# Softmax sums and the RMS factor carried to the free axis through one compact tile of bf16 parts

## The chip, the cores and the metric

The kernel runs on one core of a Trainium2 chip. The metric is the time of one execution on the device in microseconds, the median of several executions. TensorE (PE) multiplies matrices, VectorE (DVE), ScalarE (ACT) and GpSimd (POOL) do elementwise work, and SyncE (SP) issues all DMA transfers from one queue. "PEld" in the profile is TensorE's loading of weights.

## The reference

Four graph layers run over 32 independent graphs (batches) of 512 nodes with 256 features. Each layer is followed by a residual sum and a layer norm.

```python
# layer 0: attention with 8 heads of 32, masked by the adjacency
scores = where(adj > 0, q @ k.T / sqrt(32), NEG)
x = ln(x + (softmax(scores) @ v) @ Wo + bo)
# layer 1
h = (1 + eps1) * x + adj @ x
x = ln(x + relu(h @ W11 + b11) @ W12 + b12)
# layer 2
h = (eps2 * x + adj @ x) @ W21 + b21              # 1024 wide
h = h * rsqrt(mean(h ** 2, -1) + 1e-6) * rms_w
x = ln(x + silu(h) @ W22 + b22)
# layer 3
xn = layernorm(x) * gamma + beta
L  = I - s_out[:, None] * adj * s_in[None, :]      # s: 1 / sqrt(degree)
x  = ln(x + softplus(xn @ W_self + L @ xn @ W_neigh))
```

All data is fp32. The two places of this change are the division by the softmax sums (one sum for each node and head) and the multiplication by the RMS factor (one for each node).

## The kernel before, in words

One graph's 512 nodes are four tiles of 128 rows (NT = 4), its 256 features two tiles of 128 (DC = 2), and four heads share a tile of 128 features (HPG = 4). For each graph the function `graph` records its operations, stage by stage: the transposed loads of adjacency and x (`adjT`, `xT`), `qk`, `v`, the attention of four heads at a time (`attend(0)`, `attend(1)`), `wo` and the layer norm, then the first layer's `agg1`, `w11`, `w12`, the second's `agg2`, `w21`, `rms`, `silu`, `w22`, and the last layer's `x3T`, `pz`, `lap` and `softplus`.

The names that the steps below use:

- `sc` (L766): scores of four heads for 128 nodes, four matmuls of 32 rows each, in the form 32*128. L790 (DVE) masks them and finds the row minima, L804 (ACT) takes the exponential and writes its row sums to `rs`. L840 (DVE) transposes blocks in place, and L852/L864 (SP) move the tile `pq` out to DRAM (`via`) and back as `pT`.
- `po_att` (L883): probabilities times v for a pair of node tiles, 128*32 form. It holds the unnormalised result with features on partitions and nodes on the free axis.
- stage `rinv` (L903 to L957): the sums lie with nodes on partitions, and are needed along the free axis. The reciprocal `rv` (L903) is split into three bf16 parts (L912, L919), set into a zeroed 128-column tile `parts` for each node tile, transposed by four TensorE transposes (`pm_t`, L930), copied to SBUF (`mT`, L937/L938), and spread over each head's 32 partitions by one bf16 matmul of 512 columns with a selector (`pr_r`, L943). The result is copied to `oT` (L532/L533) and multiplied with `po_att` (L955). This runs once for each of the two groups of heads.
- `wo`: the matmuls `po<-wo,oT` (L970). Of two matmuls for a node tile, the second reads the second group's `oT`.
- `adjT` in graphs after the first: four loads (L580), two block transposes on VectorE (L614), a pass for the degrees on ScalarE (L624). Two buffers of adjT alternate, so a graph's loads wait for `lap` (`pa_l`, L1411) of the graph two before.
- `pg` (L1165) is the 1024-wide product of layer 2, copied by VectorE (L1220) or ScalarE (L1226); ScalarE squares it (L1241) and GpSimd adds the squares up (`ssq`, L540).
- stage `rms`: `pm` (L1251) sums the squares over partitions with nodes on the output's partitions, L1263 makes the mean, GpSimd the power -1/2 (`rr`, L558). Four VectorE products of the identity with `rr` make diagonal tiles `diag` (L1275), and one fp32 matmul of 512 columns with a matrix of ones spreads them (`pb`, L1281). Eight VectorE operations multiply by it (L1289).

The order of the work is not the order of recording. The class `Order` is a planner: each recorded operation carries a cost and, sometimes, two ways (VectorE or ScalarE). `Order.run` places operations greedily, engine by engine. An operation's rank is its due time:

```python
keys[o.n] = b * period + d - (self.HASTE if b == max(by_b) else 0)
```

Here `d` mixes the earliest and latest start within one graph (weight `LATE`) and adds `LEAD[stage]`, a number for each stage. The planner knows the buffers of each pool (four PSUM banks of tag "m"), the cost `TURN` of a change of array form on TensorE, and that VectorE operations marked `port` and GpSimd's long operations exclude each other. What it returns is emitted in that order, so several graphs are interleaved on each engine, and each engine then runs its own queue in order.

Of the kernel before, what the change touches and what calls it, by code (L numbers as in the profile page):

```python
# [9 lines left out]
F32 = mybir.dt.float32  # L10
BF16 = mybir.dt.bfloat16
AF = mybir.ActivationFunctionType
ALU = mybir.AluOpType
# [3 lines left out]
P = 128  # L17
# [2 lines left out]
RMS_EPS = 1e-6  # L20
HEADS = 8

PERIOD = 55957
LEAD = {
    "adjT": 178900, "agg1": 2600, "agg2": -164100, "degree": 73600, "diag": -115600,
# [4 lines left out]
}  # L30


# [27 lines left out]
class Order:  # L60
# [8 lines left out]
    WAIT = 70  # L69
    TABLE, TABLE_DUE = 1300, 9000  # L70

    TURN = {"whole": 93, "row": 200, "col": 93}
    TURN_DUE = 6000
    LATE = 0.85
    HASTE = 12445

    def __init__(self):
        self.ops = []
# [204 lines left out]
def kernel(  # L283
# [53 lines left out]

    ident_b = const.tile([P, P], BF16, name="ident_b")  # L340
    nc.vector.tensor_copy(ident_b, ident)
    parts = []
    for i in range(2):
        t = const.tile([P, NT, P], BF16, name=f"parts{i}")
        nc.gpsimd.memset(t, 0.0)
        parts.append(t)
    id_js = ident.rearrange("p (j s) -> p j s", s=HD)
    block = const.tile([P, HPG], F32, name="block")
    nc.vector.tensor_reduce(block, id_js, axis=AX.X, op=ALU.add)
    rows_js = const.tile([P, HPG], F32, name="rows_js")  # L350
    nc.vector.tensor_reduce(rows_js, id_js[:, :, 0:3], axis=AX.X, op=ALU.add)
    rows_of = const.tile([P, 1], F32, name="rows_of")
    nc.vector.tensor_reduce(rows_of, rows_js, axis=AX.X, op=ALU.add)
    sel_r = const.tile([P, HPG, HD], BF16, name="sel_r")
    nc.vector.tensor_scalar_mul(
        sel_r, block.unsqueeze(2).to_broadcast([P, HPG, HD]), rows_of[:, 0:1]
    )

    order = Order()

# [138 lines left out]
    def graph(b):  # L499
# [26 lines left out]
        def either(r, w, dve_way, act_way, port=False):  # L526
            op([("DVE", dve_way[0], dve_way[1], {"port": 1} if port else {}), ("ACT", act_way[0], act_way[1], {})], r, w)
# [32 lines left out]
        def small(name, bufs=2, shape=None):  # L560
            return Buf(sb, shape or [P, NT], F32, "s_" + name, f"{name}_{b}", bufs)
# [186 lines left out]

        oT = tmp([P, DC, N], "oT", 1)

        def attend(g):


            mx = small("mx", 2, [P, NT, HPG])
            rs = small("rsum", 2, [P, NT, HPG])
            po = bank("po_att")
            pTs = []
            for t in range(NT):
# [21 lines left out]
                for j in range(HPG):  # L780

                    if early:
                        row = lambda pq=pq, j=j: pq().rearrange(
                            "p a j c s -> p (a j c s)"
                        )[:, j * N : (j + 1) * N].rearrange("p (a n) -> p a n", a=4)
                    else:
                        row = lambda pq=pq, j=j: pq[:, :, j].rearrange("p a c s -> p a (c s)")
                    dve(
                        780,
                        lambda t=t, j=j, sc=sc, row=row: nc.vector.tensor_tensor_reduce(  # L790
                            out=row(),
                            in0=sc[:, j, :].rearrange("p (a n) -> p a n", a=4),
                            in1=bias[:, t, :].rearrange("p (a n) -> p a n", a=4),
                            scale=-1.0,
                            scalar=3.0e38,
                            op0=ALU.add,
                            op1=ALU.min,
                            accum_out=mx[:, t, j : j + 1],
                        ),
                        [(sc, j), (bias, t)], [(pq, j), (mx, t, j)],  # L800
                    )
                    act(
                        800,
                        lambda t=t, j=j, row=row: nc.scalar.activation(  # L804
                            row(), row(), AF.Exp,
                            bias=mx[:, t, j : j + 1],
                            scale=-1.0,
                            accum_out=rs[:, t, j : j + 1],
                        ),
                        [(mx, t, j)], [(pq, j), (rs, t, j)],  # L810
                        table="exp",
                    )
                stage[0] = "move"
# [81 lines left out]
                )  # L895

            stage[0] = "rinv"

            tj = [(t, j) for t in range(NT) for j in range(HPG)]
            rv = small("rv", 2, [P, NT, HPG])  # L900
            dve(
                240,
                lambda: nc.vector.reciprocal(rv(), rs()),  # L903
                [(rs, t, j) for t, j in tj], [(rv,)],
            )
            part = parts[g].rearrange("p t (j s) -> p t j s", s=HD)
            left = rv
            for r in range(3):
                dst = part[:, :, :, r]
                dve(  # L910
                    190,
                    lambda dst=dst, left=left: nc.vector.tensor_copy(dst, left()),  # L912
                    [(left,)], [("parts", g), ("parts", g, r)], port=True,
                )
                if r < 2:
                    rest = small("rest", 2, [P, NT, HPG])
                    dve(
                        180,
                        lambda dst=dst, left=left, rest=rest: nc.vector.tensor_tensor(  # L919
                            rest(), left(), dst, ALU.subtract  # L920
                        ),
                        [(left,), ("parts", g, r)], [(rest,)], port=True,
                    )
                    left = rest
            pm_t = Buf(ps, [P, N], BF16, "m", f"pm_t_{b}", 4)
            mT = tmp([P, N], "mT", 2, dtype=BF16)

            def tr():
                for t in range(NT):
                    nc.tensor.transpose(  # L930
                        pm_t[:, t * P : (t + 1) * P], parts[g][:, t, :], ident_b
                    )

            pe(240, tr, [("parts", g)] + [("parts", g, r) for r in range(3)], [(pm_t,)], mT)
            either(
                [(pm_t,)], [(mT,)],
                (420, lambda: nc.vector.tensor_copy(mT(), pm_t())),  # L937
                (590, lambda: nc.scalar.copy(mT(), pm_t())),  # L938
            )
            pr_r = bank("pr_r")  # L940
            pe(
                130,
                lambda: nc.tensor.matmul(  # L943
                    pr_r(),
                    lhsT=sel_r.rearrange("p j e -> p (j e)"),
                    rhs=mT(),
                    start=True,
                    stop=True,
                ),
                [(mT,)], [(pr_r,)], oT,  # L950
            )
            evacuate(lambda: oT[:, g, :], pr_r, [(pr_r,)], [(oT, g)])
            dve(
                700,
                lambda: nc.vector.tensor_tensor(oT[:, g, :], po(), oT[:, g, :], ALU.mult),  # L955
                [(po,)], [(oT, g)],
            )  # L957

        def pair_sum(lhs, lhs_k, w, w_k, nk, y, step):

# [101 lines left out]
        values()  # L1062
        attend(0)
        attend(1)
        stage[0] = "wo"
        pair_sum(oT, lambda k: (oT, k), wo, "wo", DC, y, DC)

# [211 lines left out]
        pe(  # L1279
            870,  # L1280
            lambda: nc.tensor.matmul(  # L1281
                pb(), lhsT=ones, rhs=diag().rearrange("p t q -> p (t q)"), start=True, stop=True
            ),
            [(diag,)], [(pb,)],
        )
        for m in range(C2):
            dve(
                750,
# [235 lines left out]
```

## Time and profile before

| | us |
|---|---|
| median of three runs | 3435.14 (3434.87 to 3435.78) |
| the profiled execution | 3424.53 |
| its span, first to last instruction | 3422.5 |
| VectorE busy in the span | 2664.6 |
| ScalarE busy | 2033.0 |
| GpSimd busy | 857.9 |
| TensorE granted clock | 0.998 |

Instructions of the two steps in the profiled execution (mean length of a record; records of consecutive matmuls overlap):

| line, engine | what | count | mean ns |
|---|---|---|---|
| L930 PE | pm_t, 128x128 bf16 | 256 | 219 |
| L943 PE | pr_r, 128x512 bf16 | 64 | 379 |
| L1281 PE | pb, 128x512 fp32, two passes | 64 | 639 |
| L903 DVE | reciprocal | 64 | 214 |
| L912 DVE | parts, of rv and of the rest | 64 and 128 | 637 and 185 |
| L919 DVE | rest | 128 | 175 |
| L938 ACT | mT from pm_t | 59 | 585 |
| L533 ACT | oT from pr_r | 61 | 586 |
| L955 DVE | oT times po_att | 64 | 688 |
| L1275 DVE | diag | 128 | 299 |

How to read the profile's lines: the groups give line, engine, operation, out<-in by the program's names, count, then busy time, mean length and idle time before. In the timeline the first two numbers are start and length in us, "x20" is a merged run of twenty, and brackets give the idle time before and what ended it. In the waits the numbers are total us, times and longest. An fp32 matmul of the program stands as two records (two passes). "32*128" is the form of the array, rows by columns.

### The profile page before, as it was taken

Reading aid. Unit: us, or ns where it says so; the run is one execution under the profiler, and the core shown is the slowest. Engines: PE = TensorE matmul, PEld = TensorE weight load, DVE = VectorE, ACT = ScalarE, POOL = GpSimd, SP = SyncE. Lnnn points to the kernel's source line nnn. Section 1 sums busy time; section 2 is a strip of 40 time slices with the busy share of each in tenths; the row PEclk is TensorE's granted clock in tenths of the full one; section 3 lists DMA queues with packets and bytes.
Section 4 is the critical chain, followed back from the end, with each engine's and each line's share of the span. In section 5 each row is a group of like instructions: output and inputs, shape, how many; then the busy total and the mean of one; then the engine's idle time right before and its main releaser. Section 6 shows DMA issues by size and latency. Waiting matters only on the chain.

```text
span 3422.5 us, 55733 instructions
## 1 busy us (share of the span) xinstructions
PE 3368.0 (98%) x20000; PEld 2030.2 (59%) x20000; DVE 2664.6 (78%) x6241; ACT 2033.0 (59%) x4124; POOL 857.9 (25%) x615
## 2 busy tenths in 40 slices
PE   8999999999999999999999999999999999999997
PEld 5556655665655666556655655565566655565565
DVE  7788878778777788777787777887877877778755
ACT  6555666556666556666566655666565666556633
POOL 1222222222232222222132321222222223212231
PEclk9999999999999999999999999999999999999999
DMA  5777766667767667666677666676766767766710
GB/s 152 231 220 215 207 195 191 197 186 213 198 186 199 194 197 202 195 189 197 187 212 198 186 191 200 194 204 190 197 191 191 215 191 196 192 196 180 207 40 13
DMA packets 622868, 644.74 MB, mean 188 GB/s; under 512 B 410752, under 2 KB 446976, under 8 KB 590848
## 3 DMA queue, kind: packets, MB, share of 16 engines
q1 hardware_dynamic: 622592, 641.19, 66.9%
q8 instruction: 157, 2.57, 0.3%
q14 instruction: 119, 0.97, 0.1%
HBM read 364.27 MB, written 276.82 MB: 187 GB/s over the span
## 4 chain that ended last, share of the span: by engine, by line
PE 89%; DMA 5%; DVE 3%; issue 1%; SPq 1%; ACT 1%; POOL 0%; DVEq 0%; POOLq 0%
PE po L970 22%; PE ph L1148 13%; PE pg L1165 7%; PE sc L766 7%; PE pq L694 7%; PE pa L1165 7%; PE pz L1369 7%; PE pa_l L1411 6%; PE po_att L883 6%; DMA adjT<-in_adj_dram 4%; PE pv L735 3%; PE pb L1281 1%; PE pt L1341 1%; DVE pq L790 1%; PE pm L1251 1%
## 5 line engine op out<-in xcount | busy, mean ns | idle before, releaser
L804 ACT ACTIVATE pq<-pq,mx 128x512 f32<-128x512 f32 x1024 | 728.1, 712 | 255.9 <-DVE mx L790 161.0
L790 DVE CUSTOM_DVE_ANT_0 pq<-sc,bias 128x512 f32<-128x512 f32 x1024 | 664.0, 684 | 151.0 <-PE sc L766 95.3
L840 DVE STREAM_TRANSPOSE pq<-pq 128x2048 f32<-128x2048 f32 x248 | 572.2, 2307 | 82.7 <-ACT pq L804 82.5
L970 PE MATMUL po<-w,gT 128*128 128x256 f32 x2048 | 466.6, 381 | 0.5 <-ACT gT L1304 0.5
L1165 PE MATMUL pg<-hT,w 128*128 128x512 f32 x1024 | 465.9, 598 | 0.0
L970 PEld LDWEIGHTS po<-w,gT 128*128 128x128 f32 x2048 | 384.4, 190 | 88.8 <-issue 36.9
L540 POOL TENSOR_TENSOR ssq<-ssq,sq 128x512 f32<-128x512 f32 x220 | 281.1, 1278 | 292.1 <-ACT sq L1241 285.1
L1023 POOL TENSOR_TENSOR rstd<-ve,nhalf 128x4 f32<-128x4 f32 x132 | 143.7, 1089 | 767.9 <-DVE ve L1018 767.8
L1165 PEld LDWEIGHTS pg<-hT,w 128*128 128x128 f32 x1024 | 189.4, 190 | 218.6 <-issue 206.0
L766 PE MATMUL sc<-kT,qT 32*128 32x512 f32 x2048 | 292.1, 640 | 5.3 <-DVE nmr L1030 4.4
L883 PEld LDWEIGHTS po_att<-pT,v 128*32 128x32 f32 x8192 | 215.8, 110 | 94.9 <-issue 66.8
L883 PE MATMUL po_att<-pT,v 128*32 128x128 f32 x8192 | 250.2, 274 | 0.0
L1369 PE MATMUL pz<-wsn,xnT 128*128 128x512 f32 x512 | 236.7, 597 | 0.4 <-DVE xnT L1352 0.4
L540 POOL TENSOR_TENSOR sp<-sp,y 128x1024 f32<-128x1024 f32 x31 | 73.0, 2355 | 645.6 <-PE pg L1165 572.5
L1165 PE MATMUL pa<-hT,w 128*128 128x512 f32 x512 | 233.3, 599 | 0.3 <-DVE hT L532 0.3
L1148 PE MATMUL ph<-adjT,y_att 128*128 128x512 f32 x512 | 227.3, 596 | 1.4 <-DVE adjT L1130 1.4
L1148 PE MATMUL ph<-adjT,y 128*128 128x512 f32 x512 | 228.5, 598 | 0.0
L970 PE MATMUL po<-w,aT 128*128 128x256 f32 x1024 | 227.6, 379 | 0.0
L1411 PE MATMUL pa_l<-zy,adjT 128*128 128x256 f32 x1024 | 226.6, 379 | 0.0
L1411 PEld LDWEIGHTS pa_l<-zy,adjT 128*128 128x128 f32 x1024 | 194.5, 190 | 40.8 <-issue 15.5
L970 PEld LDWEIGHTS po<-w,aT 128*128 128x128 f32 x1024 | 192.0, 190 | 26.5 <-ACT pq L804 0.8
L804 ACT ACTIVATION_READ_ACCUMULATOR pq<-pq,mx 128x1 f32 x1024 | 191.9, 187 | 0.0
(150 smaller groups left out, 4991.6 us busy)
## 6 DMA issues: line engine op xcount, KB each, us to landing
via<-pq SPq DMA_DIRECT2D x992, 256.0 KB, 4.3
pT<-via SPq DMA_DIRECT2D x248, 1024.0 KB, 5.7
adj<-in_adj_dram SPq DMA_DIRECT2D x32, 1024.0 KB, 5.1
adjT<-in_adj_dram SPq DMA_DIRECT2D x124, 256.0 KB, 4.7
x<-in_x_dram SPq DMA_DIRECT2D x32, 512.0 KB, 3.9
xT<-in_x_dram SPq DMA_DIRECT2D x124, 128.0 KB, 4.1
out_dram<-sp SPq DMA_DIRECT2D x31, 512.0 KB, 5.2
w<-in_L_gnn_W_dram SPq DMA_DIRECT2D x2, 1024.0 KB, 6.5
```

What stands on the lines that cost most here:

```text
L540: lambda: nc.gpsimd.tensor_tensor(dst(), dst(), src(), ALU.add), {},
L694: nc.tensor.matmul(pq(), lhsT=w[:, c, m * P : (m + 1) * P], rhs=xT[:, c, :], start=(c == 0), stop=(c == DC - 1),)
L766: nc.tensor.matmul(sc[:, j, :], lhsT=qT[hp, g, t * P : (t + 1) * P], rhs=kT[hp, g, :], start=True, stop=True,)
L790: lambda t=t, j=j, sc=sc, row=row: nc.vector.tensor_tensor_reduce(out=row(), in0=sc[:, j, :].rearrange("p (a n) -> p a n", a=4), in1=bias[ ...
L804: lambda t=t, j=j, row=row: nc.scalar.activation(row(), row(), AF.Exp, bias=mx[:, t, j : j + 1], scale=-1.0, accum_out=rs[:, t, j : j + 1],),
L840: lambda pq=pq: nc.vector.transpose(pq().rearrange("p a j c s -> p (a j c s)"), pq().rearrange("p a j c s -> p (a j c s)"),),
L883: nc.tensor.matmul(po[j * HD : (j + 1) * HD, t * P : (t + 1) * P], lhsT=v[:, c, h * HD : (h + 1) * HD], rhs=pT[:, :, j, c, :], start=(c == 0),
L970: nc.tensor.matmul(po[:, i * D : (i + 1) * D], lhsT=lhs[:, k, t * P : (t + 1) * P], rhs=w[:, k, :], start=(i == 0 and k == 0), stop=(i == ...
L1148: nc.tensor.matmul(ph(), lhsT=xin[:, m, c * P : (c + 1) * P], rhs=adjT[:, m, :], start=(m == 0), stop=(m == NT - 1),)
L1165: nc.tensor.matmul(pa(), lhsT=w[:, c, m * P : (m + 1) * P], rhs=hT[:, c, :], start=(c == 0), stop=(c == DC - 1),)
L1369: nc.tensor.matmul(pz(), lhsT=xnT[:, c, t * P : (t + 1) * P], rhs=wsn[:, c, :], start=(c == 0), stop=(c == DC - 1),)
L1411: nc.tensor.matmul(pa[:, i * D : (i + 1) * D], lhsT=adjT[:, m, t * P : (t + 1) * P], rhs=zy[:, m, D : 2 * D], start=(m == 0), stop=(m == N ...
```

## The change

All sums of both head groups are kept in one tile `rs` [128, 2, 4, 4]. `po_att` is copied to `oT` as soon as it is done. After both groups, `normalise` takes one reciprocal of 32 columns, splits it into three bf16 parts side by side (96 columns), transposes them with one TensorE transpose, and spreads them by eight bf16 matmuls of 128 columns (four for each group), each with its own selector. The product then reads the spread sums from PSUM and `oT` from SBUF. For the RMS factor, `split` makes 12 columns of parts, one transpose gives 12 rows, and four bf16 matmuls of 128 columns over 12 rows take the place of `diag` and the fp32 matmul. The planner's parameters are others too, so all engines' orders are planned anew; among the results, the first load in the DMA queue is x, and the adjT loads and transposes stand elsewhere.

```diff
-PERIOD = 55957
+PERIOD = 71805
 LEAD = {
-    "adjT": 178900, "agg1": 2600, "agg2": -164100, "degree": 73600, "diag": -115600,
-    "lap": -139200, "ln0": -34000, "ln1": -303400, "ln2": 108900, "ln3": 310600, "load": 67000,
-    "move": -461200, "pv": -4100, "pz": -65900, "qk": 9400, "rinv": -98900, "rms": -72400,
-    "scores": -4600, "silu": 110900, "softplus": 52400, "v": 134300, "w11": 4200, "w12": -5600,
-    "w21": -3500, "w22": -9100, "wo": -16600, "x3T": -71100, "xT": -89500,
+    "adjT": 1500, "agg1": -8100, "agg2": -16500, "degree": 64500, "diag": 111900, "lap": -94700,
+    "ln0": 5100, "ln1": 18700, "ln2": 16800, "ln3": 26700, "load": 6200, "move": 1300,
+    "pv": 5300, "pz": 15400, "qk": 7900, "rinv": -300, "rms": 100, "scores": -700,
+    "silu": -28600, "softplus": 46100, "v": 28700, "w11": -34100, "w12": -56500, "w21": 5500,
+    "w22": -8500, "wo": -32400, "x3T": -25400, "xT": -36000,
 }
...
-    TURN = {"whole": 93, "row": 200, "col": 93}
-    TURN_DUE = 6000
-    LATE = 0.85
-    HASTE = 12445
+    TURN = {"whole": 93, "row": 290, "col": 150}
+    TURN_DUE = 7000
+    LATE = 1.06
+    HASTE = 24152
...
+            evacuate(lambda: oT[:, g, :], po, [(po,)], [(oT, g)])
+
+        def split(src, n, name):
+
+            parts = tmp([P, 3, n], "p_" + name, 2, name + "p", dtype=BF16)
+            left, left_k = src, []
+            for r in range(3):
+                dve(
+                    190,
+                    lambda r=r, left=left: nc.vector.tensor_copy(parts[:, r, :], left()),
+                    [(left,)], [(parts, r)], port=True,
+                )
+                if r < 2:
+                    rest = small(name + "rest", 2, [P, n])
+                    dve(
+                        180,
+                        lambda r=r, left=left, rest=rest: nc.vector.tensor_tensor(
+                            rest(), left(), parts[:, r, :], ALU.subtract
+                        ),
+                        [(left,), (parts, r)], [(rest,)], port=True,
+                    )
+                    left = rest
+            pm_t = Buf(ps, [P, P], BF16, "m", f"pm_t_{b}", 4)
+            mT = tmp([P, P], "mT_" + name, 1, dtype=BF16)
+            pe(
+                65,
+                lambda: nc.tensor.transpose(
+                    pm_t[0 : 3 * n, :], parts().rearrange("p r x -> p (r x)"), ident_b
+                ),
+                [(parts, r) for r in range(3)], [(pm_t,)], mT,
+            )
+            either(
+                [(pm_t,)], [(mT,)],
+                (220, lambda: nc.vector.tensor_copy(mT[0 : 3 * n], pm_t[0 : 3 * n, :])),
+                (330, lambda: nc.scalar.copy(mT[0 : 3 * n], pm_t[0 : 3 * n, :])),
+            )
+            return mT
+
+        def normalise():
...
+            mT = split(rv, NX, "sums")
+            for g in range(2):
+                pr_r = bank("pr_r")
+
+                def spread(g=g, pr_r=pr_r):
+                    for t in range(NT):
+                        x = (g * NT + t) * HPG
+                        nc.tensor.matmul(
+                            pr_r[:, t * P : (t + 1) * P],
+                            lhsT=sel_r[0 : 3 * NX, x : x + HPG].rearrange("p j e -> p (j e)"),
+                            rhs=mT[0 : 3 * NX],
+                            start=True,
+                            stop=True,
+                        )
+
+                pe(240, spread, [(mT,)], [(pr_r,)])
                 dve(
...
+                    700,
+                    lambda g=g, pr_r=pr_r: nc.vector.tensor_tensor(
+                        oT[:, g, :], pr_r(), oT[:, g, :], ALU.mult
+                    ),
+                    [(pr_r,)], [(oT, g)],
+                )
...
         attend(0)
         attend(1)
+        normalise()
...
-        diag = tmp([P, NT, P], "sq", 2, "diag")
-
-        def spread():
+        mT = split(rr, NT, "rms")
+        pb = bank("pb")
+
+        def spread_rms():
             for t in range(NT):
-                nc.vector.tensor_scalar_mul(diag[:, t, :], ident, rr[:, t : t + 1])
+                nc.tensor.matmul(
+                    pb[:, t * P : (t + 1) * P],
+                    lhsT=sel_t[0 : 3 * NT, t],
+                    rhs=mT[0 : 3 * NT],
+                    start=True,
+                    stop=True,
+                )
 
-        dve(880, spread, [(rr,)], [(diag,)])
-        pb = bank("pb")
-        pe(
-            870,
-            lambda: nc.tensor.matmul(
-                pb(), lhsT=ones, rhs=diag().rearrange("p t q -> p (t q)"), start=True, stop=True
-            ),
-            [(diag,)], [(pb,)],
-        )
+        pe(240, spread_rms, [(mT,)], [(pb,)])
```

The selectors `sel_r` and `sel_t` are made once, at the start, from the identity.

More of the change, by code (lines that the diff above doesn't have):

```diff
@@ L341, with selector @@
     nc.vector.tensor_copy(ident_b, ident)
[L342 to L356, printed above, removed]
-    )
+    def selector(n, wide, name):
+        of = const.tile([P, n], F32, name=f"{name}_of")
+        nc.vector.tensor_reduce(
+            of, ident[:, 0 : 3 * n].rearrange("p (r x) -> p x r", r=3), axis=AX.X, op=ALU.add
+        )
+        sel = const.tile([P, n, wide], BF16, name=name)
+        nc.vector.tensor_copy(sel, of.unsqueeze(2).to_broadcast([P, n, wide]))
+        return sel
+    NX = 2 * NT * HPG
+    sel_r = selector(NX, HD, "sel_r")
+    sel_t = selector(NT, P, "sel_t")
     order = Order()
@@ L749, in graph @@
         oT = tmp([P, DC, N], "oT", 1)
+        rs = small("rsum", 2, [P, 2, NT, HPG])
         def attend(g):
             mx = small("mx", 2, [P, NT, HPG])
-            rs = small("rsum", 2, [P, NT, HPG])
             po = bank("po_att")
@@ L807, in attend @@
                             scale=-1.0,
-                            accum_out=rs[:, t, j : j + 1],
+                            accum_out=rs[:, g, t, j : j + 1],
                         ),
-                        [(mx, t, j)], [(pq, j), (rs, t, j)],
+                        [(mx, t, j)], [(pq, j), (rs, g, t, j)],
                         table="exp",
@@ L897, in attend @@
             stage[0] = "rinv"
-            tj = [(t, j) for t in range(NT) for j in range(HPG)]
-            rv = small("rv", 2, [P, NT, HPG])
-            dve(
-                240,
-                lambda: nc.vector.reciprocal(rv(), rs()),
-                [(rs, t, j) for t, j in tj], [(rv,)],
-            )
[L906 to L909, printed above, removed]
-                dve(
-                    190,
-                    lambda dst=dst, left=left: nc.vector.tensor_copy(dst, left()),
-                    [(left,)], [("parts", g), ("parts", g, r)], port=True,
-                )
[L915 to L920, printed above, removed]
-                        ),
-                        [(left,), ("parts", g, r)], [(rest,)], port=True,
-                    )
-                    left = rest
@@ L925, in attend @@
[L925 to L939, printed above, removed]
@@ L940, in attend @@
-            pr_r = bank("pr_r")
-            pe(
[L942 to L957, printed above, removed]
+            evacuate(lambda: oT[:, g, :], po, [(po,)], [(oT, g)])
@@ new lines, in normalise @@
+        def normalise():
+            stage[0] = "rinv"
+            rv = small("rv", 2, [P, NX])
+            dve(
+                240,
+                lambda: nc.vector.reciprocal(rv(), rs().rearrange("p g t j -> p (g t j)")),
+                [(rs, g, t, j) for g in range(2) for t in range(NT) for j in range(HPG)],
+                [(rv,)],
+            )
+            mT = split(rv, NX, "sums")
[12 more added lines that the diff above has]
+                pe(240, spread, [(mT,)], [(pr_r,)])
+                dve(
+                    700,
[3 more added lines that the diff above has]
+                    [(pr_r,)], [(oT, g)],
+                )
@@ L1269, in graph @@
         rsqrt(rr, ms, [(ms,)], [(rr,)])
-        diag = tmp([P, NT, P], "sq", 2, "diag")
-        def spread():
+        mT = split(rr, NT, "rms")
+        pb = bank("pb")
+        def spread_rms():
             for t in range(NT):
-                nc.vector.tensor_scalar_mul(diag[:, t, :], ident, rr[:, t : t + 1])
-        dve(880, spread, [(rr,)], [(diag,)])
-        pb = bank("pb")
-        pe(
-            870,
-            lambda: nc.tensor.matmul(
-                pb(), lhsT=ones, rhs=diag().rearrange("p t q -> p (t q)"), start=True, stop=True
-            ),
-            [(diag,)], [(pb,)],
-        )
+                nc.tensor.matmul(
[6 more added lines that the diff above has]
+        pe(240, spread_rms, [(mT,)], [(pb,)])
         for m in range(C2):
```

## The prediction

> **What bounds the kernel now.** I read the page first: busy shares, the slices, the chain that ended last.
>
> ```profile
> PE 3368.0 (98%) x20000; PEld 2030.2 (59%) x20000; DVE 2664.6 (78%) x6241; ACT 2033.0 (59%) x4124; POOL 857.9 (25%) x615
> ...
> PEclk9999999999999999999999999999999999999999
> ...
> PE 89%; DMA 5%; DVE 3%; issue 1%; SPq 1%; ACT 1%; POOL 0%; DVEq 0%; POOLq 0%
> ```
>
> TensorE is busy 98% of the span at full clock and carries 89% of the chain. So an edit counts by what it takes from TensorE's queue and by the waits it makes or removes there. VectorE at 78% is the engine that can be late. A busy matmul record is longer than the matmul's share of the queue, so I price by start-to-start distances in TensorE's timeline, here from one batch in the middle (start, length, line):
>
> ```profile
> 1605.81 8.85 PE L1165 MATMUL pg<-hT,w 128*128 128x512 f32 x20
> 1614.59 1.14 PE L766 MATMUL sc<-kT,qT 32*128 32x512 f32 x8
> 1615.66 1.96 PE L883 MATMUL po_att<-pT,v 128*32 128x128 f32 x64
> ...
> 1633.45 1.13 PE L1281 MATMUL pb<-diag,ones 128*128 128x512 f32 x2
> 1634.42 7.03 PE L1148 MATMUL ph<-adjT,y_att 128*128 128x512 f32 x16
> ...
> 1650.26 0.39 PE L930 MATMUL pm_t<-ident_b,parts 128*128 128x128 bf16 x4
> 1650.49 1.95 PE L970 MATMUL po<-w,gT 128*128 128x256 f32 x8
> 1652.27 0.38 PE L943 MATMUL pr_r<-mT,sel_r 128*128 128x512 bf16 x1
> 1652.48 1.89 PE L970 MATMUL po<-w,gT 128*128 128x256 f32 x8
> ```
>
> In the individual records an fp32 pass of 512 columns takes 0.429 us. Twenty pg passes are then 8.58, and the run lasts 8.78: the 0.20 over is 0.10 for a weight load not hidden after a change of array form, and 0.09 for the change to sc's 32*128. So entering a tiled form costs 0.09, returning to 128*128 costs 0.20. Four pm_t take 0.22 (0.056 each, with new weights for each), pr_r 0.21, pb 0.97, of which 0.10 is the reload after sc that the next matmul inherits: 0.86.
>
> Then the waits (total us, times, longest), TensorE's first:
>
> ```profile
> PE po L970 <- DVE oT L955: 16.9, 19, 3.7
> ```
>
> ```profile
> DVE adjT L614 <- DMA adjT<-in_adj_dram: 55.0, 28, 4.1
> ...
> DVE pq L790 <- DMA adjT<-in_adj_dram: 46.5, 19, 2.6
> ```
>
> The one large wait of TensorE in the body is wo's for oT. VectorE's timeline shows why: the product is queued behind a transpose that stands waiting for its loads.
>
> ```profile
> 2037.36 2.37 DVE L614 STREAM_TRANSPOSE adjT<-adjT 128x1024 f32<-128x1024 f32 x2 [4.07 <-DMA adjT<-in_adj_dram]
> ...
> 2040.85 0.69 DVE L955 TENSOR_TENSOR oT<-po_att,oT 128x512 f32<-128x512 f32 x1
> ```
>
> Gaps over normal spacing between wo matmuls add up to 23.5 us in the records, some 5 of them weight loads: 18 us of wait over 32 batches. Last the head:
>
> ```profile
> 4.04 2.04 PE L453 MATMUL bvwo<-wo,bv_c 128*128 128x256 f32 x4 [4.04 <-DMA wo<-in_L_gnn_Wo_dram]
> ...
> 7.58 0.43 SPq L393 DMA_DIRECT2D x<-in_x_dram  x1
> ...
> 11.78 1.94 PE L651 MATMUL pt<-ident,x 128*128 128x128 f32 x8 [5.69 <-DMA x<-in_x_dram]
> ```
>
> **The change, part by part. TensorE's work.** Removed per batch: eight pm_t transposes 0.45, two pr_r 0.43, pb 0.86: 1.74 us. Added: one 96-column transpose 0.06, eight 128-column bf16 spreads 8 x 0.056 = 0.45, one 12-column transpose 0.06, four 12-row spreads X. The last two are not whole-array work. In the built program the 12-column transpose has a 128x32 tile and the 12-row spreads a 32x128 tile, which the planner books as "whole". In 28 of 32 batches the new order is pq, transpose, sc, spreads, po_att, where form changes are due anyway, so the pair adds one change: 0.09. X is not in the trace. Its lower end is pm_t's spacing, 0.22, below which four 128-column matmuls cannot go. sc speaks for more: its two passes of 0.43 take 1.07 - 0.09 = 0.98, so about 0.10 of weight load per pass is not hidden in that form. bf16 loads (98 ns in the group rows) are half as long as fp32 ones (190), so I take 0.05 for each: X = 0.42. The Trainium skill speaks against the change here: "TensorE: Matmul & The Clock Gate", section "The mechanism", says that a weight load overlaps running matmuls only where the row group differs, and all four spreads sit in one. With that page's columns / 1.2 ns ("LDWEIGHTS"), an estimate of 107 ns, X would be 0.65. pm_t's 56 ns with new weights each time shows hidden loads in the whole form; no row shows bf16 in the 32-row form. Sums: gain 0.86 (X low), 0.66 (mine), 0.43 (rule) per batch, times 32: 27.5, 21, 14 us. All form changes counted in the two orders are 678 and 715; the five beyond the 32 above cost 0.5 us.
>
> **VectorE and ScalarE.** VectorE loses two split chains (3.1 us) and four diag products (0.9), gains one reciprocal, ten small split operations of about 0.18, two small copies of mT, and two copies of po_att to oT at 0.69: about level at 82.7 of 105 us per batch. ScalarE loses two mT and two oT copies (2.3 us) but table loads rise from 129 to 185: 56 x 1.28 = 72 us over the kernel, at a share of 59%. Neither sum is on the path while TensorE has work queued; without that cover the tables would cost 2.2 us a batch. The copies of po_att come before the product, so oT is ready one copy later. Between the last po_att and wo stand pq (1.9) and half of pv (0.9), and wo's first pass 0.43: 3.2 us, against latency 0.25 + copy 0.69 + one score pass 0.61 + product 0.69 = 2.2. It fits.
>
> **The moved order.** LEAD and PERIOD are new, so all is replanned. The adjT transposes stood about 15 us after the end of lap, when the loads land. Now the second layer's ph (6.9), a score group and rv precede them, and the queue issues four adjT loads together instead of three, two pT, one. By durations VectorE reaches them at about 15 us with loads landed by 11 to 13. The pT loads now behind adjT are needed 24 us after lap. What was late becomes early: I credit the 18 us in full. What is late next: the bf16 parts of the sums before the 96-column transpose, and the rms parts before theirs. Counted from the end of lap, TensorE reaches the former at 6.9 + 1.1 + 1.9 + 13.9 + 1.9 = 25.7 us. On VectorE the scores are there at 8.2, four score passes at 0.61 end at 10.6, copy of po_att and bias at 11.7, the first pg copy (ready at 12.0) at 12.7, L840 at 15.0; then two adjT transposes 2.4, three pg copies 2.0, four statistics 2.2, and rv, bias, diagonal and five parts 2.0: 23.6. Slack 2 us. But GpSimd adds squares in this stretch, and a cast caught beside it is long:
>
> ```profile
> L912 DVE CAST parts<-rv 128x16 bf16<-128x16 f32 x64 | 40.8, 637 | 0.0
> ```
>
> Its median is 193 ns, 26 of 64 ran beside GpSimd at about 1.4 us, and the later parts ran clear (185). The Trainium skill, "SBUF — State Buffer", section "Who interferes with whom", says that two-input SBUF operations and fast-mode casts on VectorE fully block against a reading GpSimd. By the row one cast of five is hit, +0.44, inside the slack: no wait. By the rule all five are at risk: seven adds of 1.28 fill 9 of about 12 us, 0.75 x 0.64 = 0.5 each, 2.4 in all, 0.4 of wait. pm and the rms parts have similar small slacks. I take 0.3 us per batch, 9 us; ends 0 and 1.3 (40 us), the upper one all five hit for a whole 1.28 less the slack, with part of it absorbed by later slack.
>
> **The head.** The queue now issues x first instead of eleventh, so x should land near 0.7 + 4 = 5 us instead of 11.8: 7 us, less bvwo (0.9), which lay in that wait and moves into the body: -6, ends -7 and -2. The tail's operations are the same but for rms: 0, plus or minus 4.
>
> **Sum.** -21 (-27 to -13.5), -18 (to 0), -6, +9 (0 to 40): -36. The profiled execution took 3424.5 us (span 3422.5 and 2 around it), and becomes 3388.5; the median of 3435.1 is 10.6 above it for reasons outside the trace, so I move it by the same difference: about 3400.
>
> **Rivals.** (1) No new wait and hidden loads: -27 - 18 - 6 = -51, 3384; for it, the slack counts; against it, the port row. (2) Waits one for one: new waits of 0.6 to 1 us a batch eat wo's 18 us and some more: 3409 to 3422; for it, three short slacks in one stretch. (3) Slower: the parts are blocked behind GpSimd's adds each batch, and TensorE, in order, stands before the 96-column transpose with pq, pm and the next scores queued behind it. The gain is 45 us, or 1.4 us a batch, so this decides from there; at 1.8 us it costs 58 and gives 3448. For it, the rule; against it, 2 us of slack and casts half of which escaped. (4) Nearly no change: the same wait at 1.2 to 1.6 us.
>
> **Chances.** Forecast (3391 to 3412) 0.57; (1) 0.13; (2) beyond 3412 0.15; (4) 0.07; (3) 0.08. A measurement of this kernel tells 0.2% (7 us) from no change: faster 0.85, same 0.07, slower 0.08. The range 3384 to 3431 leaves out half of (1), all of (3) and most of (4): 0.065 + 0.08 + 0.05, about 0.2.
>
> **What would show it.** pb gone and the 12-row spreads 0.4 us from start to next start; no wo wait for oT beyond 3 us in all; adjT transposes without a load wait; first transpose of x near 5 us; a wait of the 96-column transpose for its parts under 0.3 us a batch. A batch period near 103.8 us instead of 105 is the whole of it. I am wrong if that transpose or pm waits over a microsecond, or if wo waits as before.

## The result and the profile after

The changed kernel takes 3389.78 us (median of four runs, 3385.40 to 3392.58); the kernel before, measured beside it, 3435.46 (3434.87 to 3437.59). The ratio is 0.987, with a 95% interval of 0.9855 to 0.9886: 45.7 us faster. The forecast was 3400, the range 3384 to 3431. The time lies inside the range, and just under the forecast's own 3391 to 3412.

The profiled execution took 3385.40 us (span 3383.6), 39.1 less than the profiled one of before. The medians differ by 45.7. That the two differences are not equal turns out to matter. Busy times on the page:

```profile
PE 3336.5 (99%) x20064; PEld 2029.4 (60%) x20064; DVE 2806.0 (83%) x6170; ACT 2037.7 (60%) x4091; POOL 864.2 (26%) x613
```

TensorE is still the bound. VectorE, which I had called level, is 141 us busier. TensorE's timeline, again from one batch in the middle (start, length):

```profile
1600.27 0.22 PE L924 MATMUL pm_t<-ident_b,rmsp 128*12 128x128 bf16 x1
1600.42 1.14 PE L766 MATMUL sc<-kT,qT 32*128 32x512 f32 x8
1601.38 0.38 PE L1288 MATMUL pb<-mT_rms,sel_t 12*128 12x128 bf16 x4
1601.69 1.95 PE L883 MATMUL po_att<-pT,v 128*32 128x128 f32 x64
...
1697.18 0.26 PE L924 MATMUL pm_t<-ident_b,sumsp 128*96 128x128 bf16 x1
...
1699.86 0.61 PE L953 MATMUL pr_r<-mT_sums,sel_r 96*128 96x128 bf16 x8
1700.31 1.94 PE L693 MATMUL pq<-xT,wk 128*128 128x512 f32 x4
```

The four 12-row spreads stand 0.31 us ahead of po_att, with the change of form (0.09) in it: X is 0.22, its lower end. The eight spreads of the sums take 0.45, as priced. One period later the rms transpose comes again at 1703.89, so a batch takes 103.62 us (104.52 before, from pb to pb in the batch shown there).

TensorE's waits (total us, times, longest) no longer contain wo for oT. A new one heads the list:

```profile
PE ph L1160 <- DVE y L1052: 8.9, 28, 0.3
PE pt L650 <- DMA x<-in_x_dram: 5.3, 1, 5.3
...
PE po_att L883 <- DMA pT<-via: 4.6, 3, 3.7
PE pm L1263 <- POOL ssq L539: 2.3, 2, 2.0
...
PE pm_t L924 <- DVE sumsp L907: 0.6, 1, 0.6
```

By the distances between records the ph wait is larger than this row: the first matmul of ph starts 28 times 0.48 us later than its usual spacing, 13.5 us. VectorE's timeline, with GpSimd and TensorE, shows how it comes about:

```profile
1665.51 1.01 POOL L1034 TENSOR_TENSOR rstd<-ve,nhalf 128x4 f32<-128x4 f32 x1 [16.66 <-DVE ve L1029]
1667.64 0.48 DVE L1433 SCALAR_TENSOR_TENSOR zy<-pa_l,ns_out,zy 128x256 f32<-128x256 f32 x1 [2.21 <-PE pa_l L1422]
1668.05 2.30 DVE L840 STREAM_TRANSPOSE pq<-pq 128x2048 f32<-128x2048 f32 x1
1670.27 0.44 DVE L1433 SCALAR_TENSOR_TENSOR zy<-pa_l,ns_out,zy 128x256 f32<-128x256 f32 x1
1670.63 0.15 DVE L1041 SCALAR_TENSOR_TENSOR nmr<-mv,rstd 128x4 f32<-128x4 f32 x1
...
1671.38 1.96 PE L1160 MATMUL ph<-adjT,y 128*128 128x512 f32 x4 [0.32 <-DVE y L1052]
```

GpSimd has rstd ready at 1666.52. The small nmr that needs it stands on VectorE behind two zy that wait for lap's products and behind a 2.30 us block transpose, and runs only at 1670.63. TensorE waits for the y after it. VectorE is not short of time here: it idles 2.21 us just before.

VectorE's own wait of the adjT transposes for their loads went from 55.0 us to 1.5, and that of the mask passes is gone. At the head, the first transpose of x starts at 5.27 us (11.78 before) and the first q product at 7.14 (13.65 before):

```profile
5.27 1.94 PE L650 MATMUL pt<-ident,x 128*128 128x128 f32 x8 [5.27 <-DMA x<-in_x_dram]
```

But TensorE's waits in the first 300 us are only about 2 us less in all than before (21 to 23 us against 22 to 25, by where one draws the line for a gap): po_att now waits for pT (3.9), pv for VectorE (2.4), pm for GpSimd (2.2).

### The profile page after: what moved, and what is told of

It is laid out like the page before. It is cut to its first block, busy times and chain, and to the rows that moved or that the text cites. A ratio compares the mean times of both kernels' runs of the same rounds, so it can differ in the third digit from the quotient of the medians.

```text
span 3383.6 us, 55754 instructions
## 1 busy us (share of the span) xinstructions
PE 3336.5 (99%) x20064; PEld 2029.4 (60%) x20064; DVE 2806.0 (83%) x6170; ACT 2037.7 (60%) x4091; POOL 864.2 (26%) x613
## 4 chain that ended last, share of the span: by engine, by line
PE 92%; DVE 4%; DMA 1%; SPq 1%; ACT 1%; issue 1%; POOL 0%; POOLq 0%; DVEq 0%
PE po L981 23%; PE ph L1160 13%; PE pg L1177 12%; PE sc L766 8%; PE po_att L883 7%; PE pq L693 7%; PE pz L1380 7%; PE pa L1177 7%; PE pa_l L1422 4%; PE pv L734 4%; DVE pq L840 2%; PE pt L1352 1%; PE pm L1263 1%; DVE zy L1433 1%; SPq L579 0%
## 5 line engine op out<-in xcount | busy, mean ns | idle before, releaser
L1034 POOL TENSOR_TENSOR rstd<-ve,nhalf 128x4 f32<-128x4 f32 (+1 forms) x132 | 136.3, 1033 | 1273.4 <-DVE ve L1029 1256.1
L1177 PE MATMUL pg<-hT,w 128*128 128x512 f32 x1024 | 448.9, 595 | 1.4 <-DVE gT L1232 1.4
L539 POOL TENSOR_TENSOR ssq<-ssq,sq 128x512 f32<-128x512 f32 x220 | 295.8, 1344 | 63.3 <-ACT sq L1253 51.6
L1160 PE MATMUL ph<-adjT,y_att 128*128 128x512 f32 x512 | 234.2, 592 | 0.0
L1380 PE MATMUL pz<-wsn,xnT 128*128 128x512 f32 x512 | 229.4, 601 | 0.4 <-DVE xnT L1363 0.4
L1300 DVE SCALAR_TENSOR_TENSOR gT<-gT,rw_c,pb 128x512 f32<-128x512 f32 x256 | 186.1, 742 | 0.8 <-PE pb L1288 0.6
```

Source lines behind the costliest of these rows:

```text
L539: lambda: nc.gpsimd.tensor_tensor(dst(), dst(), src(), ALU.add), {},
L1160: nc.tensor.matmul(ph(), lhsT=xin[:, m, c * P : (c + 1) * P], rhs=adjT[:, m, :], start=(m == 0), stop=(m == NT - 1),)
L1177: nc.tensor.matmul(pa(), lhsT=w[:, c, m * P : (m + 1) * P], rhs=hT[:, c, :], start=(c == 0), stop=(c == DC - 1),)
L1380: nc.tensor.matmul(pz(), lhsT=xnT[:, c, t * P : (t + 1) * P], rhs=wsn[:, c, :], start=(c == 0), stop=(c == DC - 1),)
```

## The experiments

Twelve kernels. Each time is a median; e1 to e4 ran on one chip, e5 and e6 on another, e7 to e10 on a third, e11 and e12 on a fourth. The kernel before gave medians of 3428.7, 3430.9, 3432.4 and 3430.4 there. The changed kernel, once more and unedited, is e10:

> The changed kernel once more, unedited, beside the others on one chip, so that the small differences (5 to 15 us) stand against a run of the same chip: 3385 to 3393.

It took 3389.36 us (3388.61 to 3390.01). I compare with 3389.4 below. For e1 to e4 and e12 that is a comparison across chips, so here are also the lengths of a batch in the profiles (from pz to the next batch's pz on TensorE, median of 25 batches in the middle). They show what a kernel gains or loses in every batch, whatever its start:

| kernel | us a batch |
|---|---|
| before | 104.63, shortest 104.10 |
| e5 | 104.96 |
| e7 | 104.10 |
| the changed kernel, in its first profile and in e10 | 103.63 |
| e1 | 103.85 |
| e2 | 104.48 |
| e3 | 103.85 |
| e4 | 103.07 |
| e9 | 103.62 |

e10 also has a second profile of the changed kernel, and its start differs from the first one's. Here are the first profile, then e10's, at the same place in the order:

```profile
249.44 1.98 PE L693 MATMUL pq<-xT,wk 128*128 128x512 f32 x4
...
254.49 1.95 PE L883 MATMUL po_att<-pT,v 128*32 128x128 f32 x64
```

```profile
250.97 1.05 PE L1263 MATMUL pm<-ones,ssq 128*128 128x1 f32 x8 [2.12 <-POOL ssq L539]
...
252.36 3.68 PE L693 MATMUL pq<-xT,wk 128*128 128x512 f32 x4
...
259.11 1.95 PE L883 MATMUL po_att<-pT,v 128*32 128x128 f32 x64
```

e10 is 4.6 us later at this po_att, and that is the whole difference of the two spans (3383.6 and 3388.2). 1.7 us of it are the four k products, 3.68 us long in place of 1.98: right behind TensorE's waits (1.2 us for the parts, then 2.3 for ssq) its granted clock between 251 and 257 us was 0.72, while in the first profile, with waits of 0.7 and 2.2, it stayed 1.00. So the first profile, the fastest of its four runs, has a favourable start, and the 2 us that its head gains are a loss of about 2 in e10.

**What TensorE's work is worth: e1 and e2.** In e1 the spreads are issued twice, in e2 one fp32 matmul takes their place (the edit is in `spread_rms`):

```diff
-            for t in range(NT):
+            for t in [t for t in range(NT)] * 2:          # e1
...
+            nc.tensor.matmul(pb(), lhsT=ones, rhs=w11[:, 0, :], start=True, stop=True)   # e2, no loop
```

> The changed kernel with its order kept, in which the four 12-row spreads of the RMS factor are issued twice into the same bank. In the trace of the changed kernel they take 0.31 us from start to next start with a change of form of 0.09 in it, so hidden weight loads (X = 0.22) say: eight of them stand 0.53 us ahead of po_att, and the kernel is 0.22 x 32 = 7 us slower than the changed one, about 3397. Partly hidden loads (X = 0.42, the prediction's) say 13 us, 3403. Loads not hidden at all (the rule's 0.65) say 21 us, 3411. A rival in which TensorE has room to spare at this place says 0, 3390.

> The changed kernel with its order kept, in which one fp32 matmul of 512 columns (a matrix of ones with a tile of w11) fills pb in place of the four 12-row spreads; the RMS factor is thereby left out, its parts and their transpose are still made. If TensorE's queue is the bound and every us in it counts once, this gives back 0.86 + 0.19 (change to the whole form and reload) - 0.31 = 0.74 us a batch, 24 us: about 3413. If X were the prediction's 0.42, it would be 17 us, 3407. If the gain came from the moved waits and the head and not from TensorE's work, it is under 5 us.

e1 took 3397.24 us, 7.9 more than the changed kernel: the value for hidden loads (7), not for 13 or 21. In its timeline the eight stand 0.54 us ahead of po_att, 0.23 more than the four:

```profile
1607.61 0.61 PE L1288 MATMUL pb<-mT_rms,sel_t 12*128 12x128 bf16 x8
1608.15 1.96 PE L883 MATMUL po_att<-pT,v 128*32 128x128 f32 x64
```

e2 took 3414.52 us, 25.2 more; I had expected 24. From sc's start to po_att's the trace has 2.12 us in place of 1.27, and 0.85 x 32 is 27. The batch is 0.85 us longer too. So TensorE's work counts about one for one, and the whole-form fp32 matmul costs about what the sum had for it (0.85 a batch more than the spreads, 0.74 expected). The kernel of e2 leaves the RMS factor out.

**The parts of the sums: e3 and e9.** e3 does the last cast of the sums' parts twice; e9 shortens the adds of squares that run beside the casts, and so leaves most of the squares out:

```diff
+                    lambda r=r, left=left: [                               # e3
+                        nc.vector.tensor_copy(parts[:, r, :], left())
+                        for _ in range(2 if r == 2 and n == NX else 1)
+                    ],
...
-                add_to(ssq, sq, 1280, 690, [(sq,)], [(ssq,)])
+                add_to(lambda: ssq[:, 0:64], lambda sq=sq: sq[:, 0:64], ...)   # e9
```

> The changed kernel with its order kept, in which the last of the three casts of the sums' parts is done twice on VectorE. My reading: GpSimd's adds block about 2.5 us of this chain in a batch and the slack of 2 us ahead of the 96-column transpose is used up to 0.04 us, so each further cast (0.17 us free, 1.26 beside GpSimd) goes onto the path: 6 to 40 us slower, with a wait of TensorE at that transpose of 0.2 us or more a batch, 3396 to 3430. Rival: there is slack left at that place, and the transpose waits no longer than before: within 3 us of the changed kernel.

> The changed kernel with its order kept, in which the adds of the squares take 64 of 512 columns, on GpSimd and VectorE alike (the mean square is then wrong for most nodes). If GpSimd's reading of SBUF is what makes the casts of the sums' parts 1.25 us, they fall to about 0.17 us, the parts are ready some 2 us earlier, and TensorE's wait at the 96-column transpose (0.04 us a batch) goes; since slack had hidden the rest, the time falls by 0 to 3 us only. Rival: casts of 32 columns take 1.25 us whatever GpSimd does: they stay.

e3 took 3395.88 us, 6.5 more, the lower end. TensorE's wait at the 96-column transpose is 0.2 us in nearly every batch there, 6.2 us in all: po_att starts 2.08 ahead of the transpose, against 1.88 in the changed kernel.

```profile
1700.88 1.95 PE L883 MATMUL po_att<-pT,v 128*32 128x128 f32 x64
1702.96 0.26 PE L927 MATMUL pm_t<-ident_b,sumsp 128*96 128x128 bf16 x1
```

So the slack at this place is used up in the changed kernel: in most batches the transpose starts 0.05 to 0.09 us after the last cast ends, and 0.055 is what e3 has, where TensorE waits for that cast. Yet it hardly waits: once, 0.7 us by the spacing. What used the slack up is GpSimd. The tile's rows (min/median/max ns) of the second and third cast, in the changed kernel:

```profile
L907 DVE CAST sumsp<-sumsrest x64: 168/1252/1269, 51.2 to 3209.8; 128x32 bf16<-128x32 f32 x64
```

and in e9, with adds of 64 columns in place of 512:

```profile
L907 DVE CAST sumsp<-sumsrest x64: 166/174/301, 52.2 to 3211.2; 128x32 bf16<-128x32 f32 x64
```

The same instruction takes 1.25 us beside GpSimd's long adds and 0.17 without. Of the 64 casts of this row 53 took over a microsecond, and each of these ended 0.04 us after an add of ssq had ended. In e9's batch the parts are ready 2.0 us before TensorE comes to them. Yet e9 took 3386.59 us, only 2.8 less: nearly all of the blocking had fitted into the slack of 2 us, though VectorE became 100 us less busy:

```profile
PE 3338.4 (99%) x20064; PEld 2030.4 (60%) x20064; DVE 2706.0 (80%) x6170; ACT 2033.3 (60%) x4091; POOL 636.8 (19%) x613
```

**The new wait at ph: e4.** One move in the emitted order: nmr and VectorE's y of the first layer norm go ahead of the VectorE operations that were emitted between rstd and nmr.

```diff
+            rstd, nmr, ys = ln[5], ln[6], ln[7:]
+            i, j = out.index(rstd), out.index(nmr)
+            first = next((o for o in out[i + 1 : j] if o.way[0] == "DVE"), None)
...
+            go = [nmr] + [o for o in ys if o.way[0] == "DVE"]
...
+            k = out.index(first)
+            out[k:k] = go
```

> The changed kernel with one move in its order: VectorE's nmr and y of the first layer norm stand ahead of the zy operations and the block transpose that wait for lap, behind which they were queued. My reading: TensorE's wait at the first matmul of the second layer's ph (28 times 0.48 us) comes from that queueing alone, so it goes and the kernel takes about 13 us less, 3376. Rival: the wait is set by the layer norm's own chain (statistics, GpSimd's power) or turns into a wait of the same size at lap or the next scores: 3387 to 3393.

e4 took 3374.52 us, 14.9 less than the changed kernel and 0.9838 (0.9816 to 0.9860) of the kernel before: the version that beats both. Its batch is 0.56 us shorter: the wait of 0.48 and smaller gaps of the ph matmuls right behind it. The wait is gone from TensorE's list and nothing took its place; nmr now follows the first zy's place directly:

```profile
1664.51 0.48 DVE L1447 SCALAR_TENSOR_TENSOR zy<-pa_l,ns_out,zy 128x256 f32<-128x256 f32 x1 [2.21 <-PE pa_l L1436]
1664.91 0.15 DVE L1055 SCALAR_TENSOR_TENSOR nmr<-mv,rstd 128x4 f32<-128x4 f32 x1
...
1667.76 4.45 PE L1174 MATMUL ph<-adjT,y 128*128 128x512 f32 x10
```

In this batch one zy still comes first; it was the block transpose behind it that had to be passed.

**The wait of wo: e5 and e7, on the kernel before.** e5 moves the two adjT transposes behind the product in the emitted order. e7 keeps the order and loads adjT as whole rows:

```diff
-                    [("SP", 5800, lambda q=q: load_blocks(adjT(), adj[b], q), ...
+                    [("SP", 5800, lambda q=q: nc.sync.dma_start(
+                        adjT()[32 * q : 32 * q + 32],
+                        adj[b].rearrange("(m p) c -> p m c", p=P)[32 * q : 32 * q + 32],
+                    ), ...
```

> The kernel before with one move in its order: the two block transposes of adjT (L614) and what depends on them stand behind the second group's product (L955) on VectorE, in the graphs after the first. My reading: the wait of wo for oT, 18 us in the records, comes from the product being queued behind a transpose that waits for its loads, so the kernel takes about 17 us less, 3418. Rival: another wait of the same size takes its place (the scores' masks read adjT and come later): 3433 to 3437.

> The kernel before with its order kept, in which the adjT loads of the graphs after the first fetch the same bytes as whole rows of 2 KB in place of 128-byte pieces (the later block transposes then leave a scrambled adjacency in adjT: only the time is of interest). The loads should land earlier, so that the transposes L614 and the mask passes find them there. My reading, that wo's wait for oT and the scatter of the runs of before both come from these landings: wo's wait falls under 5 us, the kernel takes about 20 us less than before (18 us of wait in the profiled run, some 10 more in a median run), near 3410, and its runs lie within 5 us of each other. Rival from the run in which the transposes were moved behind the product: VectorE is late in this stretch by its own work, the wait moves to the next scores: 3425 to 3433.

e5 took 3432.60 us, 1.0006 (0.9998 to 1.0014) of before: nothing gained. wo's wait went, and the scores of the next graph began to wait for a mask pass on VectorE instead:

```profile
PE sc L790 <- DVE mx L814: 23.0, 30, 0.9
...
PE po L994 <- DVE oT L979: 2.8, 2, 2.7
```

In the kernel before that row of sc is 0.9 us:

```profile
PE sc L766 <- DVE mx L790: 0.9, 1, 0.9
```

In the batch that I looked at VectorE is nearly full from the product to those passes, so as I read it the move only handed the 2.4 us of the transposes on. My reading of e5 fell; its rival was right.

e7 took 3402.55 us, 0.9913 (0.9899 to 0.9926): 29.9 less than before, more than the 20 expected, and wo's wait is 0.2 us. Its adjacency is scrambled, so only its time counts. The rows of the loads (issue ns min/median/max), of before and of e7, each with the time from issue to landing:

```profile
L580 SPq DMA_DIRECT2D adjT<-in_adj_dram x124: 593/1172/3363, 42.2 to 3284.8; - x124
DMA to landing us min/median/max: 3.2/4.7/10.5
```

```profile
L608 SPq DMA_DIRECT2D adjT<-in_adj_dram x124: 316/430/2162, 41.4 to 3258.9; - x124
DMA to landing us min/median/max: 3.1/4.6/10.2
...
PE po L973 <- DVE oT L958: 0.2, 1, 0.2
```

From issue to landing hardly anything changed. It is the issue that got shorter, by 0.74 us for each of four loads. The loads of before were late because SyncE took 4 x 1.17 = 4.7 us to issue them.

The profiles show what the wait was worth in one run. The gaps between wo's matmuls came to 23.5 us before, and to 0.6 in e7; in the changed kernel they are 0.1. The forecast had set 5 of the 23.5 aside as weight loads; these went too. e7's profiled run is 22.0 us faster than that of before.

The runs of e7 also lie close together, 3400.3 to 3404.2, and those of e5 have a standard deviation of 1.3 us, while the kernel before scatters with 4.2 to 5.9 (3422.7 to 3441.2 over these chips). So the scatter of before is mostly that of this wait. Four profiles of kernels with before's body agree: gaps at wo of 23.5 (before), 27.6 (e11), 27.3 (e6) and 31.4 us (e8) go with times of 3424.5, 3426.8, 3429.3 and 3436.8; e11 had won 1.8 us at its start, and e8 lost 3.3.

**The head: e6, e8 and e11 on the kernel before, e12 on the changed one.** e6, e8 and e11 reorder the start of before; e12 puts the changed kernel's first twelve loads back into the order of before:

```diff
+        ten = [self.ops[i] for i in (5, 6, 7, 18, 0, 1, 3, 4, 16, 8)] + by_b[0][:2]   # e12
+        for o in ten:
+            out.remove(o)
+        out[0:0] = ten
```

> The kernel before with another order at the start alone: x, wq, wk and the adjacency stand first in the DMA queue, and bvwo behind the first transposes of x. My reading: the first transpose starts near 5 us in place of 11.8 and the gain stays to the end, less bvwo's 0.9: 6 us less, about 3429. Rival: the time saved at the start is lost at the first load that now comes later: within 2 us of before.

> The kernel before with another order at the start alone: x, wq, wk and the adjacency first in the DMA queue, and bvwo behind the four q and k products of the first graph (in the earlier run bvwo, standing right behind the transposes of x, waited 4 us for wo and held the products up). My reading: the first q product starts at 7.1 us in place of 13.65 and the lead is kept: about 6 us less than before. Rival: the lead is lost within the first graph, whose scores and layer norm wait for VectorE (the 4.4 us wait of the scores at 87 us): the lead in TensorE's timeline is 6 us at 14 us and under 1 us at 110 us, and the time is that of before.

> The kernel before with another order at the start alone: x first in the DMA queue as in the run with bvwo later, and on VectorE the copy of xT ahead of the two operations on bq and epsilon behind which it had stood until their loads landed at 13.3 us. First q product near 7.1 us in place of 13.65. If the lead is kept to the end: about 6 us less than before, and TensorE's timeline shows the 88 us and 107 us landmarks (first ph, third pm_t) about 6 us earlier. Rival: the waits of the first graph take it back (the scores' 4.4 us wait for VectorE's nmr grows): lead under 2 us at 107 us, time within 2 us of before.

> The changed kernel with the order of its first twelve loads that of before (x eleventh); nothing else moves. The first transpose of x waits to about 11.8 us. If the head counts in full, the kernel is 6.5 us slower than the changed one (3389.4): 3396. Rival: the changed kernel's waits in its first 250 us (pT 3.9, pm 2.2, pv 2.4 and pg 1.6 us in TensorE's queue) hang on loads that don't move with x, and take most of it back: 1 to 3 us slower, 3391.

e6 took 3431.16 us (1.0003, 0.9995 to 1.0011) and e8 3436.17 (1.0010, 1.0002 to 1.0017). Neither did what its name says: with x early, e6's products stood behind bvwo, which waited for wo; in e8 the copy of xT stood on VectorE behind small operations on late weights, and the first q product began at 14.44 us. e11 moved those too. Its first q product starts early, but a landmark a hundred us on, the first pm_t after the first layer's products, has kept only 1.8 of the 6.6 us. From e11 and from before:

```profile
7.04 3.10 PE L721 MATMUL pq<-xT,wq 128*128 128x512 f32 x4
...
105.05 0.39 PE L957 MATMUL pm_t<-ident_b,parts 128*128 128x128 bf16 x4
```

```profile
106.82 0.39 PE L930 MATMUL pm_t<-ident_b,parts 128*128 128x128 bf16 x4
```

e11 took 3431.05 us (0.9999, 0.9988 to 1.0009): no gain that these scattering runs can tell. e12 took 3396.15 us, 6.8 more than the changed kernel, the full delay of x (first transpose at 12.12 us in place of 5.27). So x first is worth 6.8 us in the changed order and about nothing in the old one, where waits for VectorE in the first graph take the lead back.

## Why the prediction was right, and where its steps were wrong

The sign and the mechanism were right: TensorE is the bound, the change takes work from it, and wo's wait goes. The terms of the sum were off in size or in place, and their errors partly cancel, so that the number lies in the range is in part luck:

- **TensorE's work, -21.** By the added and removed instructions it was -27.5: X is 0.22, not 0.42. I had carried the 0.10 us that an fp32 pass of sc leaves uncovered over to bf16, halved. e1 shows 0.23 us for four more spreads. The rule of the Trainium skill ("TensorE: Matmul & The Clock Gate", section "The mechanism") as I applied it, 0.65 in one row group, is refuted by the same rows: the spreads follow each other at 0.056 us, in one row group and with new weights each. The same section also lets a load run ahead when it goes to the background weight buffer, which I had left out. The page's section "Weight-path perf modes — Fast Weight Load (FWL) and DoubleRow" gives the fast load to weights of 128 columns that are not fp32; the loads of the spreads took 0.09 us and fp32 ones 0.19. Why these loads hide and those of sc do not, no run here separates. As a whole TensorE's queue got shorter still: a batch without wo's wait takes 104.10 us (e7), one without ph's wait 103.07 (e4), 1.03 less in place of 0.86. Of the other 0.17 some 0.11 shows in the timelines: from the start of sc to the next matmul it is 1.07 us where po_att follows (1614.59 to 1615.66, before) and 0.96 where the bf16 spreads do (1600.42 to 1601.38). I had priced sc alike in both places.
- **wo's wait, -18, and the 10.6 us "for reasons outside the trace".** This is the largest miss. The wait is worth about 30 us in the median run (e7: 29.9). The profiled run of before was a lucky one (3424.53, where its runs lie between 3422.7 and 3441.2), with 23.4 that went, and 5 of these I had not counted. The 10.6 that I moved over unchanged were largely the same wait, which varies from run to run, and the change removes it with its scatter. In the changed kernel the median is only 4.4 above the profiled run. For the profiled run itself I had forecast 3388.5, and it took 3385.40; most of the miss of 10 us in the median is this step.
- **New waits, +9 at the parts.** The size was near, the place wrong. At the 96-column transpose TensorE waits 0.7 us in all: the slack of 2 us was worked out right (e9: 1.95). The Trainium skill's rule on blocking ("SBUF — State Buffer", section "Who interferes with whom") was the better guide for the casts: 53 of the 64 later ones were held up. The row of before (26 of 64 casts) was not the one to go by; these lay beside another add of GpSimd, y_att. The wait that came, 13.5 us, stands at ph and is one of queueing on VectorE (e4: 14.9). I had listed what the moved transposes would pass and had not looked at the layer norm behind lap.
- **The head, -6.** e12 gives 6.8 for x first. Other waits of the new start take it back: all but about 2 us in the first profile, all of it and about 2 us more in e10, where TensorE's clock fell as well.
- **VectorE about level.** It is 141 us busier. The copies to oT were in my sum. What was not is the time beside GpSimd's adds: the casts and rests of the sums' parts take 71 us more than in e9, `bias<-adj` went from a mean of 407 ns to 597 (24 us), and `y<-zy,y` from 1192 to 2810 (53 us). Before and after:

```profile
L1454 DVE SCALAR_TENSOR_TENSOR y<-zy,y 128x1024 f32<-128x1024 f32 (+1 forms) x33 | 39.3, 1192 | 1.1
L638 DVE TENSOR_SCALAR bias<-adj 128x512 bf16<-128x512 f32 x128 | 49.3, 407 | 1.6 <-DMA adj<-in_adj_dram 1.6
```

```profile
L1465 DVE SCALAR_TENSOR_TENSOR y<-zy,y 128x1024 f32<-128x1024 f32 (+1 forms) x33 | 92.7, 2810 | 1.3
L637 DVE TENSOR_SCALAR bias<-adj 128x512 bf16<-128x512 f32 x128 | 75.9, 597 | 0.0
```

e9 shows the cause for two of the three: with short adds the casts are short and `bias<-adj` is back at a median of 418 ns, none over 422. `y<-zy,y` stays at 2.8 us in e9; it lies beside another GpSimd operation, so its cause is argued from its place alone. What GpSimd's adds of squares did to VectorE cost the kernel no more than e9's 2.8 us, since TensorE had work queued.

For the two profiled runs the measured sizes give -27.5 - 23.4 - 2 + 13.5 + 0.7 = -38.7, against 39.1 measured. For the medians, with e7's 29.9 and e10's head, they give -27.5 - 29.9 + 2 + 13.5 + 0.7 = -41, against 45.7 in the first comparison and 43.1 on e10's chip. The agreement can't tell the terms apart to better than some us: the interval of e7 alone is 5 us to either side, and the 0.17 us a batch on TensorE and the small gaps behind ph's wait, which have opposite signs, are left out. What stays open: how the head's remaining waits (pT, pv, pm) divide, since no run removed them, and each half of the change (sums, RMS) with an order of its own, which was not tried. So what the new parameters alone would have gained is not shown either: wo's wait and the head belong to the new order, and of the 27.5 on TensorE only the RMS part was put back in a run (e2).

## What to carry over

When a kernel's runs scatter more than those of its neighbours, look in the trace for a wait that hangs on a DMA landing: its value in one profiled run is one draw, and here the change that removed it removed most of the scatter as well, so the gain in the median was not the gain in the trace. For a load that comes late, read the issue time in the queue beside the landing time. After a planner has moved everything, look for small instructions that another engine waits for and that stand behind a waiting or long one: moving nmr and the y behind it was worth 14.9 us, about half as much as the change's whole saving on TensorE.

## What the runs showed of the hardware

- bf16 weight loads are hidden between 128-column matmuls of 12 rows: the matmuls start 0.056 us apart, and four more spreads cost 0.23 us (e1), while two fp32 passes of sc in the 32-row form take 0.98 us where their matmuls alone are 0.86.
- Loading the same 256 KB as 128-byte pieces or as rows of 2 KB changed the issue on the queue (1.17 and 0.43 us median) and hardly the time from issue to landing (4.7 and 4.6 us).
- A cast of 128x32 from fp32 to bf16 takes 0.17 us alone and 1.25 us when it meets a GpSimd add of 512 columns (1.34 us mean). All 53 long ones ended 0.04 us after such an add: the cast waits for the add to end.
- TensorE's granted clock was 0.72 over 6 us behind two waits of 1.2 and 2.3 us (e10), and passes of 512 columns stood 0.85 us apart there in place of 0.43. Behind waits of 0.7 and 2.2 us it stayed 1.00. Where the limit lies, these runs don't show.
